# Product 3 of a batch's result in seven block products, in a cross-attention kernel of nested Strassen products

## The chip, the cores and the metric

The kernel runs on one core of a Trainium2 chip, in 32-bit floating point. The time is the device's, in microseconds, from the start to the end of one execution. The kernel before took 664.79 us (median of three runs, 664.58 to 664.88).

## The reference

Eight batches are computed with the same weights. x1 and x2 hold 512 channels x 1024 positions per batch.

```python
q = einsum('bcn,dc->bnd', x1, Wq) + bq          # 64 wide
k = einsum('bcn,dc->bdn', x2, Wk) + bk[:, None]
v = einsum('bcn,dc->bdn', x2, Wv) + bv[:, None] # 512 channels
attn = softmax(einsum('bnd,bdm->bnm', q, k), axis=2)
out = einsum('bcm,bnm->bcn', v, attn) + x1
```

## The kernel before, in words

The kernel does not form v. It multiplies x2 by the transposed exponentials of the scores first, y = x2 . e, scales y by one over the sums, and then takes the result, Wv . y + bv + x1. Both large products of a batch, y and the result, are cut into 2 x 2 blocks and done in seven products instead of eight (the Winograd form of Strassen's scheme, `MULT`, L436). The left sums S1 to S4 and the right sums T1 to T4 that they need are built by VectorE, by ScalarE with an accumulating transfer (a negation on ScalarE, then a transfer on POOL's queue that adds the other summand), or by transfers alone. Products 1, 6, 7, 5, 3 and 4 share two pairs of PSUM banks, "a" and "c"; between them ScalarE copies the partial sums of products 1, 6, 5 to buffers `tmp` that the four blocks 11, 12, 21, 22 are put together from (`evict_y`, `evict_o`).

Most of the fourteen products are themselves done in seven block products (L537 `right_stream` and L522 `left_stream` build the sums, `inner_product`, L548, issues the matmuls). Such a product uses a PSUM bank `chain` and a bank `third`: block product 1 starts the chain and is copied by ScalarE to the first half of a bank; 6 and 5 go on with the chain and are copied too; 2, 3 and 4 are added into the copies; block product 7 goes to `third`, is copied to SBUF, and VectorE adds it to the second bank at the end (`complete`, the join). A block product is one matmul of 256 columns for the result and two for y. A plain product of the result is four matmuls of 512 columns.

In the middle batches the result's products run in this order on TensorE: 4 of y and 1 of the result woven together (`multiply_41`, L788), 6 and 2 plain, then 5, 7 and 3 woven (`multiply_57`, L674; 7 in blocks, 5 and 3 plain), then 4 plain. Product 3 goes into banks "a", on top of 1, 6 and 5; block 12 is evicted from these banks by two activations of ScalarE (L930) while product 4 runs. Then the next batch begins: its product 1 of y (`multiply_seeded`, L723), 2, 6, its next batch's scores, 5, 7, 3. Only in the last batch is product 3 of the result done in blocks (`multiply_573`, L588).

All orders are written out by hand: `period(s, n, nn, nnn)` (L1168) issues the work of batch s together with that of the following ones, with `manual_schedule`. Each engine runs its instructions in the order of the program. `weave` (L492) takes operations from several streams in turn. VectorE's streams at the end of a batch are: the subtraction of the maxima from the next batch's scores (`lower`, L320; one call is one score tile of a half, 128x1024), the right sums of products 7 of the result and 1 and 2 of the next y, left sums, T1, the joins and the evictions of blocks 22 and 21; then T2 and the sums of the next batch's product 6. SP's queue carries plain loads and stores. POOL's queue carries all accumulating transfers: sums of score tiles (`add_tile`, L966), S2 and S3 (`add_11`, L181), S4 (L160), T3 (L366), T4 (L361), and the addition of x1 to a block of the result before SP stores it (L942, L943).

In the code batches count from 0 and `s.six` marks 2 to 5, so these are batches 3 to 6 here; `s.b` is the number, and `n` the batch that follows.

Of the kernel before, what the change touches and what calls it, by code (L numbers as in the profile page):

```python
# [15 lines left out]
def kernel(  # L16
# [77 lines left out]

    def load_values():
# [28 lines left out]
    class Batch:  # L124
        def __init__(self, b):
            self.b = b
            self.a, self.e, self.t, self.y, self.o = {}, {}, {}, {}, {}
            self.mx, self.top, self.den, self.few, self.rden, self.row = {}, {}, {}, {}, {}, {}
            self.tmp, self.bank = {}, {}
            self.inner = {}  # L130
            self.six = 2 <= b < B - 2
            self.one = b >= 1

# [438 lines left out]
    def left_values(i, k):  # L572

        x = w[k]
        inner_w[i] = v = {f"{p + 1}{q + 1}": x[:, q : q + 1, ts(p, P)] for p in range(2) for q in range(2)}
        if i == "o3":
            sums = sb.tile([P, 4, 1, P], F32, tag="aS1", name=f"w_I{k}")
        else:
            sums = const.tile([P, 4, 1, P], F32, name=f"w_I{k}")
        for z, (k, x, y, op) in enumerate(LEFT):  # L580
            v[k] = sums[:, z]
            nc.vector.tensor_tensor(v[k], v[x], v[y], op)
            yield
# [89 lines left out]
    def multiply_57(s, hook):  # L673
# [10 lines left out]
        s.tmp[5] = sb.tile([P, 2, H], F32, tag="u5", name=f"uo5_{s.b}")  # L684

# [36 lines left out]

    def multiply_seeded(s, i, v_tag, hooks={}, bank=None):  # L723
# [10 lines left out]
        chain, third = inner_parts(s, i)  # L734
        if v_tag == "top" or s.b == B - 1 and v_tag == "r":
# [172 lines left out]
    def evict_o(s, k, hook=None, rows=range(2)):  # L908
# [5 lines left out]
        if s.b == B - 1 and k == "12":  # L914
            bank = "d"
        r, h = int(k[0]) - 1, int(k[1]) - 1
# [94 lines left out]
    def head(s):  # L1011
# [13 lines left out]
        warm = const.tile([P, P], F32, name="warm")  # L1025
# [86 lines left out]
    def period(s, n, nn, nnn):  # L1112
# [122 lines left out]
        else:  # L1235
            complete_1 = multiply_seeded(s, 1, "y11", {4: lambda: copied_s4(s)} if s.b > 1 else {})
            early = s.b > 1 and n is not None
            complete_1()
            sum_e(s, *(("T2",) if early else ("T1", "T2")))
# [42 lines left out]
            if early:  # L1282
# [8 lines left out]
            if n:  # L1291
                weave(left_stream(s, 7, s.a["S3"], "yT4"))
            if s.six:
# [55 lines left out]
            sums_4 = (left_stream(s, 4, s.a["22"], "a12"), right_stream(s, 4, s.t["T4"], "eT2"))  # L1349
# [49 lines left out]
        if five:  # L1399
# [3 lines left out]
            highest(n, 1)  # L1403
            next(products, None)
            if nn is None:
# [15 lines left out]
        if five:  # L1421
            if nn is None:
# [3 lines left out]
                in_turn(lowers(n, 0, 2, MH), lowers(n, 1, 0, 2)),  # L1426
                right_stream(s, "o7", s.y["T3"], "eT1"),
# [18 lines left out]
        if five:  # L1446
# [14 lines left out]
        if n is None:  # L1461
            weave(left_values("o3", "S4"))
# [23 lines left out]
        if n is None:  # L1486
            pass
        elif late:
# [3 lines left out]
        if n:  # L1492
            leave = evict_o(s, "22")
        if five:
            exponentials(n, 1, 3)
# [6 lines left out]
        if five:  # L1502
# [4 lines left out]
        if n:  # L1507
            weave(
                in_turn(
                    right_stream(n, 1, n.e[0][:, 0], "yT1", "yT2"), right_stream(n, 2, n.e[0][:, 1], "eT4")  # L1510
                ),
                left_stream(n, 2, n.a["12"], "aI3" if n.b > 1 else "aS4"),
            )
            if s.b == 0:
                second(3)
            last = evict_o(s, "12")
            if five:
# [3 lines left out]
            second(4)  # L1521
            total(n, 0)
            evict_o(s, "21")
# [45 lines left out]
```

## Time and profile before

| | |
|---|---|
| median of three runs | 664.79 us (664.58 to 664.88) |
| the profiled execution's own time | 664.86 us |
| its span, from the first to the last instruction of the program | 662.8 us |
| granted TensorE clock | 1.00 |
| transfers in the span | 135.88 MB |

PE is TensorE's matmuls, PEld its weight loads, DVE VectorE, ACT ScalarE, POOL GpSimd, SP the synchronisation engine. A row of a timeline gives the start in us from the span's start, the duration, the engine, the line of the kernel, the operation, what it writes and reads (tile names without their numbers), the shape and a count. Durations of neighbours on one engine overlap, so the spacing of starts is what one costs. A bracket tells how long the engine was idle before it and what ended that. The names: `i1chain`, `i6third` and the like are the banks of y's block products; `io7chain` those of the result's product 7; `e` the exponentials, `eT` their sums, `a` and `aS` the parts of x2 and their sums, `aI` the inner left sums, `y` and `yT` the blocks of y and their sums, `oa` and `oc` the banks of the result, `uo`, `r` and `o` its blocks in SBUF.

### The profile page before, as it was taken

To read this page: it belongs to the slowest core of one execution; us is meant where nothing else is said; L and a number is where in the kernel's file an instruction comes from. 1 tells how busy PE (TensorE), PEld (TensorE's weight loads), DVE (VectorE), ACT (ScalarE), POOL (GpSimd) and SP (SyncE) were. 2 spreads that over 40 slices of the span, in tenths; PEclk is the share of its full clock that TensorE was granted. 3 is DMA by queue.
4 is the path that set the end of the run, shared out by engine and by line. 5 is a ranking of instruction groups with operands and counts; after the bars stand their busy time and mean duration, and the time that the engine had idled before them with its cause. 6 is when DMAs were issued, how large, how long until landed. Compare 5 with 4: busy or idle time off the path is not lost.

```text
span 662.8 us, 7971 instructions
## 1 busy us (share of the span) xinstructions
PE 657.8 (99%) x2620; PEld 432.4 (65%) x2620; DVE 615.9 (93%) x865; ACT 378.2 (57%) x723; POOL 224.1 (34%) x192
## 2 busy tenths in 40 slices
PE   9999999999999999999999999999999999999997
PEld 4435754757658666687666786676865757666865
DVE  1989999999999989998999989999899999999997
ACT  3755456446475574655756647656577555574332
POOL 0125215631255411563125531265214640244300
PEclk9999999999999999999999999999999999999999
DMA  9688587995899859999599985999947995399504
GB/s 327 260 274 261 126 247 136 197 229 199 263 167 227 238 169 285 174 233 239 166 279 186 259 222 164 257 194 234 279 87 173 207 256 190 75 183 240 125 23 150
DMA packets 51545, 135.88 MB, mean 205 GB/s; under 512 B 5680, under 2 KB 6192, under 8 KB 51504
## 3 DMA queue, kind: packets, MB, share of 16 engines
q0 software_dynamic: 24512, 61.94, 50.7%
q1 hardware_dynamic: 26848, 73.29, 30.5%
q8 instruction: 21, 0.34, 0.2%
q10 hardware_dynamic: 144, 0.14, 0.1%
q14 instruction: 20, 0.16, 0.1%
HBM read 87.83 MB, written 16.81 MB: 158 GB/s over the span
## 4 chain that ended last, share of the span: by engine, by line
PE 98%; DMA 1%; DVE 0%; issue 0%
PE ps_yc L555 9%; PE ps_oc L464 8%; PE ps_ya L555 7%; PE ps_s L236 6%; PE ps_oa L689 6%; PE ps_oa L464 5%; PE ps_ya L464 4%; PE ps_q L191 4%; PE ps_i5chain L555 3%; PE ps_i4b L840 3%; PE ps_k L191 3%; PE ps_i3chain L555 3%; PE ps_i7chain L555 3%; PE ps_oc L840 3%; PE ps_i2chain L555 3%; PE ps_i1chain L555 3%
## 5 line engine op out<-in xcount | busy, mean ns | idle before, releaser
L331 ACT ACTIVATE e<-e 128x1024 f32<-128x1024 f32 x60 | 63.4, 1058 | 30.2 <-DVE e L322 29.2
L322 DVE TENSOR_TENSOR e<-e,top 128x1024 f32<-128x1024 f32 x60 | 72.6, 1218 | 2.5 <-POOL top L272 2.5
L291 POOL PARTITION_ALL_REDUCE den<-sum x16 | 52.8, 3298 | 63.9 <-DVE sum L266 59.0
L272 POOL PARTITION_ALL_REDUCE top<-max x16 | 29.9, 1867 | 97.0 <-DVE max L266 50.0
L966 POOL DMA_DIRECT2D sum<-e x21 | 25.6, 1219 | 102.9 <-ACT sum L971 39.1
L245 ACT COPY e<-ps_s 128x512 f32<-128x512 f32 x90 | 47.8, 622 | 10.1 <-PE ps_s L236 7.1
L236 PE MATMUL ps_s<-q,k 64*128 64x512 f32 (+1 forms) x188 | 46.6, 598 | 0.0
L256 DVE TENSOR_TENSOR max<-max,e 128x1024 f32<-128x1024 f32 x30 | 36.6, 1219 | 0.3
L236 PEld LDWEIGHTS ps_s<-q,k 64*128 64x128 f32 x188 | 17.5, 186 | 19.9 <-issue 17.0
L875 DVE TENSOR_TENSOR y<-y,den 128x1024 f32<-128x1024 f32 x24 | 29.2, 1221 | 0.3
L464 PE MATMUL ps_oa<-yT,w_S 128*128 128x512 f32 x64 | 28.8, 593 | 0.0
L464 PE MATMUL ps_oc<-yT,w 128*128 128x512 f32 x64 | 28.8, 592 | 0.0
L746 ACT COPY ps_yc<-ps_i7chain 128x256 f32<-128x256 f32 x32 | 11.4, 357 | 30.2 <-PE ps_i7chain L555 26.1
L307 POOL DMA_DIRECT2D den<-row x12 | 6.7, 559 | 58.7 <-DMA row<-few 39.2
L522 DVE TENSOR_TENSOR aI<-a,aI 128x256 f32<-128x256 f32 x60 | 25.2, 420 | 0.6
L522 DVE TENSOR_TENSOR aI<-a 128x256 f32<-128x256 f32 x60 | 25.8, 450 | 0.0
L191 PE MATMUL ps_q<-x_in_x_dram,wqk_sb 128*64 128x512 f32 x112 | 25.6, 598 | 0.0
L746 ACT COPY ps_ya<-ps_i5chain 128x256 f32<-128x256 f32 x32 | 11.5, 361 | 24.2 <-PE ps_i5chain L555 20.0
L746 ACT COPY ps_ya<-ps_i1chain 128x256 f32<-128x256 f32 x28 | 10.0, 357 | 24.3 <-PE ps_i1chain L555 20.6
L555 PE MATMUL ps_yc<-e,aI 128*128 128x256 f32 x92 | 23.6, 379 | 0.0
L689 PE MATMUL ps_oa<-yT,w_S 128*128 128x512 f32 x48 | 23.5, 592 | 0.0
L942 POOL DMA_DIRECT2D r<-in_x_dram x14 | 23.3, 1664 | 0.0
(348 smaller groups left out, 1836.9 us busy)
## 6 DMA issues: line engine op xcount, KB each, us to landing
x_in_x_dram<-in_x_dram SPq DMA_DIRECT2D x60, 512.0 KB, 8.2
a<-in_x2T_dram SPq DMA_DIRECT2D x32, 512.0 KB, 7.2
aS<-in_x2T_dram POOLq DMA_DIRECT2D x21, 512.0 KB, 10.5
sum<-e POOLq DMA_DIRECT2D x21, 512.0 KB, 5.3
eT<-eT POOLq DMA_DIRECT2D x16, 512.0 KB, 11.7
uo<-in_x_dram POOLq DMA_DIRECT2D x14, 512.0 KB, 9.9
r<-in_x_dram POOLq DMA_DIRECT2D x14, 512.0 KB, 9.0
out_dram<-r SPq DMA_DIRECT2D x14, 512.0 KB, 7.6
```

Of the source, the lines that this page charges most:

```text
L191: nc.tensor.matmul(ps[r, :], w_sb[:, c, :], s.x[:, c, ts(h, H)], start=(c == 0), stop=(c == CT - 1),)
L236: nc.tensor.matmul(ps[g][:, n], s.k[r, ts(i, P)], s.q[r, ts(h, H)][:, n], start=True, stop=True)
L245: nc.scalar.copy(e[:, g, i, :], ps[g])
L256: nc.vector.tensor_tensor(f, e[:, :, 0, :] if i == 1 else f, e[:, :, i, :], op)
L291: nc.gpsimd.partition_all_reduce(s.den[h], s.mx[h][:, 0, :], P, ReduceOp.add)
L322: nc.vector.tensor_tensor(e, e, top, ALU.subtract)
L331: nc.scalar.activation(e, e, AF.Exp)
L464: nc.tensor.matmul(ps, left[ka][:, k, ts(j, P)], right[kb][:, k, :], start=opens and k == 0, stop=i in (2, 3, 4) and k == n_k - 1, skip_gr ...
L522: nc.vector.tensor_tensor(v[k], v[x], v[y], op)
L555: nc.tensor.matmul(ps, s.inner[i][ka][:, k, :], s.inner[i, "t"][kb][:, k, :], start=opens and k == 0, stop=z in (2, 3, 4) and k == n_k - 1 ...
L689: nc.tensor.matmul(ps, w[ka][:, k, ts(j, P)], s.y[kb][:, k, :], start=False, stop=i == 3 and k == 1, skip_group_check=True,)
L840: nc.tensor.matmul(ps, s.inner[i][ka][:, k, :], s.inner[i, "t"][kb][:, k, :], start=opens and k == 0, stop=z in (2, 3, 4) and k == n_k - 1 ...
```

## The change

In batches 3 to 6 product 3 of the result is done in seven block products, woven with 5 and 7 in a new function, `multiply_573_early`. It has two banks of its own, `d`, from the pool of four that `chain` and `third` also come from. Block 12 is then in two parts: banks "a" (products 1, 6, 5) are evicted with the bias to `r12` right behind the seven products; the banks `d` are copied to SBUF by ScalarE (`evict_3`) and added to `r12` by a transfer on POOL's queue. The right sums of product 3 (`sums_o3`) and its left sums (`left_values("o3", "S4")`, once, in batch 3) are added to VectorE's work.

Product 4 of the result is issued inside the next batch's product 1 of y, behind its block product 7, with what belonged to it: S3's negation and transfer, block 22's transfer and store; batch total and the eviction of block 21 come behind block product 2. The right sums of the next batch's product 1 are issued ahead of the join of product 7, and those of product 2 partly behind product 1.

Moved besides: the subtraction and the exponential of score tile 2 of half 0 go earlier (ahead of `join_67`, and behind product 4 of y); the left sums of product 4 of y go ahead of product 5's join; product 5's third part goes into the tile `u5`; the inversion of half 0 goes behind product 7's left sums. The inner left sums of `w11` are partly held in place and in the tile `warm`.

```diff
+            self.three = 2 <= b < B - 2
...
+        if s.three:
+            return multiply_573_early(s, hook, b0, b1, chain, third)
...
+    ORDER573_EARLY = (
+        (5, 0), (5, 1), (7, 1), (7, 7), (5, 2), (3, 7), (3, 1), (7, 6), (7, 2), (3, 2), (3, 6),
+        (5, 3), (7, 5), (3, 4), (3, 5), (7, 4), (7, 3), (3, 3),
+    )
+    def multiply_573_early(s, hook, b0, b1, chain, third):
+        d = [ps_s.tile([P, H], F32, tag="s", name=f"ps_od{j}_{s.b}_3") for j in range(2)]
+        v = sb.tile([P, H], F32, tag="top", name=f"vo73_{s.b}", bufs=2)
+        v7, v3, copy = v[:, left], v[:, right], nc.scalar.copy
+        s.r12 = sb.tile([P, 2, H], F32, tag="r", name=f"r12_{s.b}")
+        a0, a1, d0, d1 = ([x[:, left], x[:, right]] for x in (b0, b1, *d))
+        steps = {
+            (7, 1): (chain, True, [(a0[0], chain)]),
+            (7, 7): (third, True, [(v7, third)]),
...
+            (7, 4): (a1[0], False, [(a1[1], chain)]),
+            (7, 3): (a0[1], False, []),
+            (3, 7): (d1[1], True, []),
+            (3, 1): (d1[0], False, [(d0[0], d1[0]), (v3, d1[1])]),
...
+        for j in range(2):
+            nc.scalar.activation(s.r12[:, j, :], s.bank["a", j], AF.Identity, bias=bv_sb[j])
+        def complete():
+            for b, v in ((b1, v7), (d[1], v3)):
+                b = b.rearrange("p (a n) -> p a n", a=2)
+                nc.vector.tensor_tensor(b, b, v.unsqueeze(1).to_broadcast([P, 2, H // 2]), ALU.add)
+                yield
...
+    def evict_3(s, n):
+        t = sb.tile([P, 2, H], F32, tag="y21", name=f"t3_{s.b}")
+        nc.scalar.copy(t[:, 0, :], s.d[0])
+        exponential(n, 1, 3)
+        nc.scalar.copy(t[:, 1, :], s.d[1])
+        nc.gpsimd.dma_start(s.r12, t, accum_op=ALU.add)
...
-            complete_1 = multiply_seeded(s, 1, "y11", {4: lambda: copied_s4(s)} if s.b > 1 else {})
+            hooks = {4: lambda: copied_s4(s)} if s.b > 1 else {}
+            if s.tail:
+                hooks[7] = lambda: (negate(s, "S3"), add_11(s, "S3"), s.tail[0]())
+                hooks[2] = s.tail[1]
+            complete_1 = multiply_seeded(s, 1, "y11", hooks)
             complete_1()
+            if s.tail:
+                s.tail[2]()
...
-            if early:
+            if early and not s.tail:
                 invert(s, 0)
...
+            if s.b == 2:
+                weave(left_values("o3", "S4"))
+            elif s.six:
+                inner_left(s, 4, s.a["22"], "a12")
             complete_5()
...
+            if s.six:
+                lower(n, 0, 2)
             join_67(s)
...
+            if s.six:
+                sums_o3 = right_stream(s, "o3", s.y["22"], "aI3")
+                next(sums_o3)
             next(products, None)
+            if s.six:
+                exponential(n, 0, 2)
...
-                in_turn(lowers(n, 0, 2, MH), lowers(n, 1, 0, 2)),
-                right_stream(s, "o7", s.y["T3"], "eT1"),
+                in_turn(lowers(n, 0, 2 + s.six, MH), lowers(n, 1, 0, 2)),
+                in_turn(right_stream(s, "o7", s.y["T3"], "eT1"), sums_o3),
...
+        elif s.three:
+            sums_n1 = right_stream(n, 1, n.e[0][:, 0], "yT2", "yT1")
+            weave(sums_n1)
+            next(complete_7)
...
+        if s.three:
+            next(complete_7)
+            evict_3(s, n)
...
+            if s.three:
+                n.tail = lambda: (leave(), second(4)), tail, lambda: weave(*sums_n2)
+            else:
+                second(4)
+                tail()
```

More of the change, by code (lines that the diff above doesn't have):

```diff
@@ L93 @@
     }
+    warm = const.tile([P, P], F32, name="warm")
     def load_values():
@@ L915, in evict_o, with leave @@
             bank = "d"
+        if k == "12" and s.three:
+            o = s.r12
+            def leave():
+                nc.gpsimd.dma_start(o, block(s, k, x1), accum_op=ALU.add)
+                nc.sync.dma_start(block(s, k, out), o)
+            return leave
         r, h = int(k[0]) - 1, int(k[1]) - 1
```

87 lines of the change are left out of this document (65 added, 22 removed).

## The prediction

> **What bounds the kernel now.** I read the page first, then the busy time by period, then the timeline of TensorE, and last VectorE, ScalarE and the transfers at the one place that the change touches.
>
> ```profile
> span 662.8 us, 7971 instructions
> PE 657.8 (99%) x2620; PEld 432.4 (65%) x2620; DVE 615.9 (93%) x865; ACT 378.2 (57%) x723; POOL 224.1 (34%) x192
> ...
> q0 software_dynamic: 24512, 61.94, 50.7%
> ...
> PE 98%; DMA 1%; DVE 0%; issue 0%
> ```
>
> ```profile
> 295.04:375.38 80.34, 80.34 (x329) 55.09 (x328) 75.84 (x109) 49.49 (x97) 30.01 (x27) 1.00 0.90 220
> ```
>
> The first fence is the page (its busy times and its chain), the second the row of one period (PE, PEld, DVE, ACT, POOL busy, the granted clock, the DMA share, GB/s). The chain that ended last is 98% PE, and in one period of a middle batch (80.34 us) PE is never idle. So a matmul fewer is worth its time, and nothing else gains anything. But VectorE is busy for 75.84 of the 80.34 us, and the DMA engines are at a share of 0.90. The reader is to see a bound engine with a second and a third right behind it: PE can only run ahead as far as they follow.
>
> The place is the seam of two batches. I work it out for the end of batch 3 and the start of batch 4 (260 to 296 us); the others lie a period further.
>
> ```profile
> 263.80 1.88 PE L689 MATMUL ps_oa<-yT,w_S 128*128 128x512 f32 x4
> ...
> 269.39 0.59 PE L555 MATMUL ps_oc<-eIo7eT,w 128*128 128x256 f32 x2
> ...
> 273.69 3.60 PE L464 MATMUL ps_oc<-yT,w 128*128 128x512 f32 x8
> 277.12 1.03 PE L555 MATMUL ps_i1chain<-e,a 128*128 128x256 f32 x4
> 277.99 1.03 PE L555 MATMUL ps_i1third<-eI1yT,aI 128*128 128x256 f32 x4
> ```
>
> The durations overlap, so the starts count: eight 512-wide instructions take 277.12 - 273.69 = 3.43 us, 0.43 each; four 256-wide ones take 277.99 - 277.12 = 0.87 us, 0.216 each. A matmul in the code is two of these instructions.
>
> **The change, part by part.** *Term 1, TensorE.* Product 3 was four matmuls of 512 columns: 8 x 0.43 = 3.43 us. It becomes seven of 256: 14 x 0.216 = 3.02 us. That saves 0.41 us in each of four batches: **-1.64 us**. No other matmul is added; product 4 changes only its place.
>
> A rule of the Trainium skill speaks against this ("TensorE: Matmul & The Clock Gate", section "The mechanism"): a weight load overlaps matmuls in flight only when its row group differs.
>
> ```profile
> 289.86 0.84 PEld L555 LDWEIGHTS ps_i6third<-eI6yT,aI 128*128 128x128 f32 x4
> 290.74 0.82 PEld L555 LDWEIGHTS ps_i6chain<-eI6y,aI 128*128 128x128 f32 x4
> ```
>
> Here every load fills all 128 rows and takes 0.19 us (the four of a group begin 0.22 apart and end 0.84 after the first began), and four loads with four matmuls still take 0.88 us from group to group: the loads are hidden, and the trace disagrees with the rule. By the rule six more loads a batch would add 4 x 6 x 0.19 = 4.6 us.
>
> *Term 2, VectorE after the seam.* This is where I expect part of the gain to go.
>
> ```profile
> 262.24 0.68 DVE L537 TENSOR_TENSOR eIo7eT<-yT 128x512 f32<-128x512 f32 x1
> 262.84 1.22 DVE L322 TENSOR_TENSOR e<-e,top 128x1024 f32<-128x1024 f32 x1
> 263.98 0.42 DVE L542 TENSOR_TENSOR eIo7eT<-eIo7eT,yT 128x256 f32<-128x256 f32 x1
> 264.31 1.22 DVE L322 TENSOR_TENSOR e<-e,top 128x1024 f32<-128x1024 f32 x1
> ...
> 270.53 0.69 DVE L719 TENSOR_TENSOR ps_oc<-ps_oc,vo 128x512 f32<-128x512 f32 x1
> 271.31 1.41 DVE L937 SCALAR_TENSOR_TENSOR uo<-ps_oc,wqk_sb,uo 128x512 f32<-128x512 f32 x2
> ...
> 273.77 2.43 DVE L340 TENSOR_TENSOR eT<-e,e 128x1024 f32<-128x1024 f32 x2
> 276.12 1.22 DVE L537 TENSOR_TENSOR eI1yT<-e 128x1024 f32<-128x1024 f32 x1
> ...
> 280.94 0.69 DVE L542 TENSOR_TENSOR eI2eT<-eI2eT,e 128x512 f32<-128x512 f32 x1
> 281.66 0.69 DVE L544 TENSOR_TENSOR eI2eT<-e,eI2eT 128x512 f32<-128x512 f32 x1
> ...
> 289.83 0.41 DVE L522 TENSOR_TENSOR aI<-aS,aI 128x256 f32<-128x256 f32 x1
> ```
>
> From 261 to 291 us VectorE runs without a gap; by the starts a 1024-wide operation takes 1.14 us, a 512-wide one 0.60, a 256-wide one 0.33. At 289.83 comes the third left sum of batch 4's product 6; its block product 6 loads it at 290.74, 0.50 us after the sum's end (290.24). That is all the lead VectorE has. What the change does to this streak:
> - the subtraction for score tile 2 leaves it: -1.14; two of the right sums of product 3 come in: +0.67;
> - the join of product 3's third part comes in (512 wide, as the one at 270.53): +0.60;
> - the three right sums of product 1 (1.14 + 0.60 + 0.60) move ahead of the join of product 7. This costs nothing by itself, but now that join waits. It needs the last copy of the seven products, which in the trace starts 0.63 us after block product 4 of product 7 (the row below at 270.02 against 269.39). In the new order four double matmuls and eleven block products lie before that one: 263.80 + 3.43 + 4.73 = 271.97. So the copy runs from 272.60 to 272.96 and the join starts at 272.99, while VectorE is free at 270.53 - 0.47 + 2.34 = 272.40: +0.59. Behind it on VectorE wait block 22's eviction, the last subtraction, T1 and T2;
> - small waits that now have passed: 271.31 - 270.53 is 0.18 above 0.60, T1 took 2.35 instead of 2.28, and 281.66 - 280.94 is 0.12 above 0.60: -0.37.
>
> The sum is +0.35 us: the third left sum ends at 290.59, while PE, 0.41 us earlier, wants to load it at 290.33. With 0.05 us for the signal (below: a sum ending at 260.06 frees a load at 260.11) PE stalls 0.31 us.
>
> ```profile
> 258.83 1.23 DVE L875 TENSOR_TENSOR y<-y,den 128x1024 f32<-128x1024 f32 x1
> ...
> 260.11 0.45 PEld L464 LDWEIGHTS ps_oc<-y,w 128*128 128x128 f32 x2 [0.41 <-DVE y L875]
> ```
>
> Batches 4, 5 and 6 have this product 6 in blocks behind a changed seam: 3 x 0.31 = **+0.9 us**. Bounds: nothing (if the join does not wait), and 3 x 0.9 = 2.7 us (if it waits twice as long).
>
> *Covered edits.* The rest I cost at nothing, with its cover:
>
> ```profile
> DVE ps_ya L763 <- ACT ps_ya L746: 1.5, 1, 1.5
> DVE uy L858 <- ACT uy L863: 1.3, 1, 1.3
> DVE ps_i4b L833 <- ACT ps_i4b L849: 1.0, 1, 1.0
> ```
>
> ```profile
> 269.16 0.58 ACT L698 COPY uo<-ps_oa 128x512 f32<-128x512 f32 x1
> 269.64 0.38 ACT L564 COPY ps_oc<-ps_io7chain 128x256 f32<-128x256 f32 x1
> 270.02 0.36 ACT L711 COPY ps_oc<-ps_io7chain 128x256 f32<-128x256 f32 x1
> 270.29 1.06 ACT L331 ACTIVATE e<-e 128x1024 f32<-128x1024 f32 x1
> 271.25 1.05 ACT L177 ACTIVATE aS<-aS 128x1024 f32<-128x1024 f32 x1
> ...
> 274.85 1.25 ACT L930 ACTIVATE r<-ps_oa,wqk_sb 128x512 f32<-128x512 f32 x2
> 275.99 1.05 ACT L177 ACTIVATE a<-a 128x1024 f32<-128x1024 f32 x1
> ```
>
> VectorE has three gaps in a period. The left sums of product 4 (4 x 0.33) go into the one of 1.5 us, the subtraction of tile 2 into the one of 1.3, the first right sum of product 3 (0.60) into the one of 1.0. ScalarE gets four more 256-wide and two more 512-wide copies a batch, and they meet at the seam: behind the copy of 272.60 (0.27 to the next start) follow the two activations of block 12 (0.57 each), an exponential, S2's negation (0.96 each), a copy (0.48), an exponential, a copy, and only then product 1's first copy, from 277.85 to 278.21. Product 4 (3.43 us), now between block products 7 and 6 of product 1, holds the reader of that copy off until 273.69 - 0.41 + 1.73 + 3.43 = 278.44: covered by 0.2 us, and every tenth beyond that stalls PE a tenth. What product 4 covered before, the eviction of block 12 (L930), is done during the seven products. The value sums are made once, in batch 3, and leave the last batch. With product 4 move S3's negation (0.96 on ScalarE, behind product 1's second copy and before its third, which comes 0.9 us after product 4), the transfers of S3 and of block 22, batch 4's total and block 21's eviction; on POOL S3 now goes ahead of block 22, and SP keeps its order of stores. The inversion of half 0 goes behind product 7's left sums, as the row that it reads comes later. Product 5's third part takes block 22's buffer, whose store goes out before block 12's: I count nothing.
>
> *Transfers.* A batch gets one more accumulating transfer of 0.524 MB: 61.94 MB took 50.7% of 662.8 us, so it is 2.8 us of all 16 engines; at 0.90 of 80.34 us some 8 us are free. On POOL's queue it stands behind the sum into S2 and ahead of T3's two sums, S3's, block 22's, and all behind these come later by about one transfer less what the three earlier ones of tiles 2, 3 and block 11 gained.
>
> **The sum:** -1.64 + 0.9 = -0.7 us on the profiled 664.86 us: 664.1; the median of 664.79 lies 0.1 below, which I can't tell apart. **664.1 us.**
>
> **The rivals.**
> *No stall.* If the join of product 7 doesn't wait (a copy 0.6 us earlier, or faster sums), VectorE stays 0.24 us ahead of the trace and PE 0.41 ahead of it: 0.50 - 0.05 - 0.41 + 0.24 is positive, and all of term 1 stays: 664.79 - 1.64 = 663.2 us. For it: every other lead closes. Against it: the copy stands last in the new order.
>
> *S2 late: slower.* ScalarE makes S2's negation at 271.25; now it stands behind block 12's activations and an exponential and ends at about 275.9, so POOL sends S2's transfer at 276.0, not 272.6.
>
> ```profile
> L181 POOL DMA_DIRECT2D aS<-in_x2T_dram x1: 905/905/905, 272.6 to 272.6; - x1
> DMA to landing us min/median/max: 9.0/9.0/9.0
> ...
> L966 POOL DMA_DIRECT2D sum<-e x1: 1252/1252/1252, 264.3 to 264.3; - x1
> DMA to landing us min/median/max: 4.9/4.9/4.9
> ...
> 282.77 1.06 ACT L156 ACTIVATE aS<-aS 128x1024 f32<-128x1024 f32 x1
> ```
>
> ScalarE reads S2 (L156) for S4, at 282.4 in the new time. If the transfer takes 9.0 us as now, it lands at 285.0; ScalarE, in order, holds product 2's first copy until 286.3, which block product 6 of product 2 wants at 284.5 (277.12 - 0.41, nine steps of 0.865 later): 1.9 us a batch, four times: 664.79 - 1.64 + 7.6 = 670.8 us. It decides from 7.0 us after issue (0.6 us of slack). For it: the one row of this transfer says 9.0. Against it: the three transfers ahead go out some 5 us earlier, and behind an emptier queue one took 4.9 us.
>
> *Loads not hidden:* 24 extra loads of 0.19 us in line with the matmuls give 664.79 - 1.64 + 4.6 = 667.7 us. The rows of PEld speak against it. (The rule of the Trainium skill quoted above would have it so.)
>
> *It does not come to blocks:* the new order is in place for all four batches by the code; I see no way for that.
>
> **How the numbers follow.** Forecast (a stall of 0.1 to 0.6 us in three batches, 663.5 to 665.0 us): 0.48. No stall (663.0 to 663.5): 0.28. S2 late (665.5 to 671): 0.17. A larger stall of the same streak, up to its bound of 2.7 us (665.0 to 666): 0.06. Loads not hidden: 0.01. The range goes from 662.9 to 667.0 and leaves out the upper half and more of S2 late, about 0.12 in all; the likeliest's own range is 663.5 to 665.0. A measurement of this kernel can tell about 0.2%, 1.3 us, from no change. Faster by more needs under 663.5: no stall, 0.28. Slower needs over 666.1: S2 late, the loads and a little of the larger stall, 0.20. Between: 0.52.
>
> **What would show it.** Term 1: in batches 3 to 6 fourteen 256-wide instructions of product 3, and the start of product 1 0.43 us earlier. Term 2: in batches 4 to 6 a start of product 6's block product 6 some 0.3 us late, released by VectorE, and a wait of product 7's join for ScalarE. Wrong: that load without a wait (no stall); ScalarE idle before S4's negation with a DMA as releaser (S2 late); PE waiting for ScalarE at block product 6 of product 1, where my 0.2 us of cover are thin; or 256-wide instructions further apart than 0.216 us.

## The result, and the profile after

The changed kernel took 668.01 us (median of 6 runs, 667.06 to 669.49), the kernel before 664.65 on the same chip (6 runs, 664.40 to 664.88): a ratio of 1.0053, 95% interval 1.0039 to 1.0067. It is slower by about 3.4 us; the forecast was 664.1, with a range to 667.0.

The page of the changed kernel, profiled in an execution of 668.01 us: span, busy times, POOL's queue of transfers, and the chain that ended last.

```profile
span 666.2 us, 8081 instructions
PE 658.8 (99%) x2644; PEld 436.9 (66%) x2644; DVE 629.6 (95%) x881; ACT 386.6 (58%) x747; POOL 230.1 (35%) x196
...
q0 software_dynamic: 25088, 64.04, 51.9%
...
PE 77%; DVE 11%; DMA 6%; issue 3%; POOL 2%; ACT 1%; SPq 0%; POOLq 0%
```

The busy time of one period (columns as before):

```profile
295.78:376.55 80.77, 80.44 (x336) 56.05 (x335) 79.29 (x113) 51.60 (x103) 31.51 (x28) 1.00 0.93 224
```

The chain was 98% PE; now it leaves TensorE for VectorE, transfers and POOL. TensorE's busy share hardly shows this (99% both times): a stall of some tenths lies under the modelled end of the matmul before it. VectorE went from 75.84 to 79.29 us of a period that itself grew from 80.34 to 80.77.

So I compare starts of the same matmul in the two traces. The start of y's product 1 shows term 1 alone: 273.30 us in place of 277.12. With product 4 (3.43 us, now behind it) taken off, that is 0.39 us earlier, and 0.41 with the 0.02 us by which this execution lay behind at 142 us. The same comes at each of the four seams. What comes back is at two kinds of place:

- into batches 4, 5 and 6: 0.83 us at each seam, so each is +0.42 in all;
- in batch 7: 2.55 us.

-1.64 + 3 x 0.83 + 2.55 = +3.40 us, which is the difference of the spans (666.2 - 662.8).

**The seam into batch 4.** The timeline of TensorE in the changed kernel:

```profile
273.30 1.03 PE L559 MATMUL ps_i1chain<-e,a 128*128 128x256 f32 x4
...
283.63 1.03 PE L559 MATMUL ps_i2third<-eI2eT,aI 128*128 128x256 f32 x4
284.84 1.13 PE L559 MATMUL ps_i2chain<-eI2eT,aI 128*128 128x256 f32 x4 [0.17 <-ACT ps_yc L821]
...
290.12 1.03 PE L559 MATMUL ps_i6third<-eI6yT,aI 128*128 128x256 f32 x4
291.30 0.89 PE L559 MATMUL ps_i6chain<-eI6y,aI 128*128 128x256 f32 x3
```

Between groups that follow without a wait lie 0.865 us. Here are 1.21 and 1.18: 0.34 and 0.31 us late, and 0.10 and 0.07 us more between the first two matmuls of each late group (the bracket shows only what the modelled ends leave of it). Into batches 5 and 6 both waits are in product 6, and both for VectorE. VectorE at the same place:

```profile
273.02 0.70 DVE L780 TENSOR_TENSOR ps_oc<-ps_oc,vo 128x512 f32<-128x512 f32 x1
...
281.81 0.69 DVE L270 TENSOR_TENSOR sum<-sum 128x512 f32<-128x512 f32 x1
282.41 1.40 DVE L1020 SCALAR_TENSOR_TENSOR o<-ps_oc,wqk_sb,uo 128x512 f32<-128x512 f32 x2
283.73 0.69 DVE L838 TENSOR_TENSOR ps_ya<-ps_ya,v 128x512 f32<-128x512 f32 x1
284.33 1.47 DVE L548 TENSOR_TENSOR eI2eT<-e,eI2eT 128x512 f32<-128x512 f32 x1
...
290.74 0.41 DVE L526 TENSOR_TENSOR aI<-aS,aI 128x256 f32<-128x256 f32 x1
```

The third left sum of product 6 is the row at 290.74; it ends at 291.15, not at the forecast 290.59. The row that does not fit is the one at 284.33: a 512-wide sum of 1.47 us, where the same sum of the same width took 0.69 in the trace of before. It waits for nothing that the profile names.

**Batch 7.** ScalarE, TensorE and VectorE of the changed kernel, each from its timeline:

```profile
551.99 0.37 ACT L821 COPY v<-ps_i7third 128x256 f32<-128x256 f32 x1 [2.53 <-DMA out_dram<-o]
```

```profile
552.68 1.13 PE L559 MATMUL ps_i7chain<-eI7yT,aI 128*128 128x256 f32 x4 [1.03 <-ACT ps_yc L821]
569.16 0.67 PE L915 MATMUL ps_oc<-eIo1i,w 128*128 128x256 f32 x2 [0.36 <-DVE yT L943]
579.38 2.84 PE L468 MATMUL ps_oc<-y,w 128*128 128x512 f32 x6 [0.30 <-DVE y L950]
```

```profile
558.21 1.23 DVE L950 TENSOR_TENSOR y<-y,den 128x1024 f32<-128x1024 f32 x1 [1.28 <-DMA den<-row]
```

Two late transfers stand behind it. The third part of product 7 goes to the tile `y12`, in which block 21's result still waits for its store. And the reciprocals of the softmax sums, sent to DRAM as a row and read back to all partitions, come late, so that VectorE can't scale y. By the starts TensorE loses 1.29 us at the store, 0.36 at the scores behind it, and 0.60 and 0.57 at the last two rows of the TensorE fence; 0.27 us that the kernel before lost inside product 4 of y at this place fall away. That makes the 2.55 us.

### The profile page after: what moved, and what is told of

Read it like the earlier page. It is cut to its first block, busy times and chain, and to the rows that moved or that the text cites. A ratio compares the mean times of both kernels' runs of the same rounds, so it can differ in the third digit from the quotient of the medians.

```text
span 666.2 us, 8081 instructions
## 1 busy us (share of the span) xinstructions
PE 658.8 (99%) x2644; PEld 436.9 (66%) x2644; DVE 629.6 (95%) x881; ACT 386.6 (58%) x747; POOL 230.1 (35%) x196
## 4 chain that ended last, share of the span: by engine, by line
PE 77%; DVE 11%; DMA 6%; issue 3%; POOL 2%; ACT 1%; SPq 0%; POOLq 0%
PE ps_yc L559 7%; PE ps_s L240 6%; PE ps_ya L559 5%; PE ps_oc L468 5%; PE ps_oa L468 4%; PE ps_q L195 4%; PE ps_k L195 3%; PE ps_ya L468 3%; PE ps_i5chain L559 3%; PE ps_i7chain L559 3%; PE ps_i3chain L559 3%; PE ps_i4b L915 3%; PE ps_oc L915 2%; PE ps_i4chain L915 2%; PE ps_oa L695 2%
## 5 line engine op out<-in xcount | busy, mean ns | idle before, releaser
L295 POOL PARTITION_ALL_REDUCE den<-sum x16 | 54.4, 3401 | 52.4 <-DVE sum L270 47.5
L276 POOL PARTITION_ALL_REDUCE top<-max x16 | 32.7, 2046 | 99.9 <-ACT ps_oa L928 52.3
L468 PE MATMUL ps_oa<-yT,w_S 128*128 128x512 f32 x64 | 28.8, 593 | 0.0
L526 DVE TENSOR_TENSOR aI<-a,aI 128x256 f32<-128x256 f32 x60 | 27.4, 456 | 1.0
L468 PE MATMUL ps_oc<-y,w 128*128 128x512 f32 x48 | 21.7, 594 | 0.3 <-DVE y L950 0.3
L195 PE MATMUL ps_k<-x_in_x_dram,wqk_sb 128*64 128x512 f32 x96 | 21.9, 598 | 0.0
L468 PE MATMUL ps_ya<-eT,aS 128*128 128x512 f32 x48 | 21.1, 592 | 0.0
## 6 DMA issues: line engine op xcount, KB each, us to landing
aS<-in_x2T_dram POOLq DMA_DIRECT2D x21, 512.0 KB, 10.5
eT<-eT POOLq DMA_DIRECT2D x16, 512.0 KB, 11.9
uo<-in_x_dram POOLq DMA_DIRECT2D x14, 512.0 KB, 10.5
```

The lines of the kernel that those rows point to most:

```text
L195: nc.tensor.matmul(ps[r, :], w_sb[:, c, :], s.x[:, c, ts(h, H)], start=(c == 0), stop=(c == CT - 1),)
L276: nc.gpsimd.partition_all_reduce(s.top[h], s.mx[h][:, 0, :], P, ReduceOp.max)
L295: nc.gpsimd.partition_all_reduce(s.den[h], s.mx[h][:, 0, :], P, ReduceOp.add)
L468: nc.tensor.matmul(ps, left[ka][:, k, ts(j, P)], right[kb][:, k, :], start=opens and k == 0, stop=i in (2, 3, 4) and k == n_k - 1, skip_gr ...
```

## The experiments

A number such as "+0.42" below is the change of TensorE's start against the kernel before, across one seam or batch of the profiled execution. The first 53 us, in which all kernels here are the same program, end between 0.3 us earlier and 1.4 us later than in the profile of before (waits for the first loads). That blurs the medians; the starts across a seam don't have this. In seam_6's profiled execution (671.88 us, 5.3 over its median) TensorE lies 5.65 us behind before batch 3, where nothing is changed yet, so of that trace I use only what comes later. The first theory was VectorE's amount of work for the seams, and the transfers for batch 7; the rival put the transfers behind both.

**seams_345** and **seam_6**: the change in batches 3 to 5 alone, and in batch 6 alone.

```diff
-            self.three = 2 <= b < B - 2
+            self.three = 2 <= b < B - 3        # seams_345; parts of the change that asked s.six ask s.three
+            self.three = b == B - 3            # seam_6
```

> The change in batches 3 to 5 only; batch 6 ends and batch 7 begins as before. Two theories of the loss. VectorE theory: each seam into a batch with product 6 in blocks (4, 5, 6) loses 0.83 us to VectorE's streak and wins 0.41, and batch 7 loses 2.6 us by its own seam's transfers; then here 664.65 + 3 x 0.42 = 665.9 us, and no wait in batch 7. Transfer theory (everything goes back to the added transfer): the same seams, so 665.9 too. Rival: batch 7's loss is a lag carried over from the batches before it; then it stays, and the time is 664.65 + 1.3 + 2.6 = 668.5 us.

> The change in batch 6 only, so that its seam leads into batch 7, which has no product 6 in blocks. VectorE theory and transfer theory: 0.41 won at the seam, about 2.6 lost in batch 7 (ScalarE waits for the store of block 21, VectorE for the row of the sums): 664.65 - 0.41 + 2.6 = 666.8 us. If batch 7's loss is carried over from earlier batches: 664.2 us.

Measured: 666.42 (ratio 1.0023, 1.0011 to 1.0036) and 666.57 us (1.0030, 1.0009 to 1.0052). seams_345: +0.42 at each of its three seams and no loss in batch 7. seam_6: -0.41 at the seam; batch 7 loses 0.53 us at product 2, where ScalarE had waited 1.07 us for S2's transfer, and 0.61 and 0.91 us behind the late row; the wait for the store of block 21 was not there. So batch 7's loss belongs to the seam just ahead of it.

**no_add**: without the accumulating transfer of product 3 to block 12 (the output lacks that part). **no_join**: with it, but without VectorE's join of product 3's third part (the output lacks that).

```diff
-        nc.gpsimd.dma_start(s.r12, t, accum_op=ALU.add)          # no_add
-            for b, v in ((b1, v7), (d[1], v3)):                  # no_join
+            for b, v in ((b1, v7),):
```

> The change without the accumulating transfer of the copied banks to block 12: product 3 is computed and copied, but left out of block 12. VectorE theory: the seams lose 0.83 us each as before (their streak holds the same operations), only batch 7's loss shrinks, to 0 to 0.5 us: 664.65 - 1.64 + 2.5 + (0 to 0.5) = 665.5 to 666.0 us. Transfer theory: with 2.8 us of transfer work less per batch the seams lose nothing either: 664.65 - 1.64 = 663.0 us.

> The change without VectorE's addition of product 3's third part (its block product 7 is left out of half of block 12); all transfers stay. VectorE theory: the streak is 0.60 us shorter per seam, so the stall at product 6 in batches 4 to 6 falls from 0.83 to about 0.2 us each: 668.0 - 1.9 = 666.1 us, batch 7 as in the change. Transfer theory: no difference, 668.0 us.

Measured: no_add 664.17 us (0.9987, 0.9979 to 0.9996), between the theories: 0.0 at each of the three seams, -0.41 at the last, no loss in batch 7. no_join 668.25 us (1.0046, 1.0031 to 1.0062), as the rival had it: the three seams still +0.42 each, although VectorE had a join of 0.60 us less to do, and batch 7 loses 2.29 us, all of it at the wait for the store. With that the theory of VectorE's amount fell. At the seam into batch 4, about 0.32 us of the time saved went into a wait of VectorE for an exponential of ScalarE (two sums start 1.45 us apart in place of 1.13). What had become of the rest shows where VectorE meets POOL. First no_join, then no_add, each with POOL's all-reduce of the batch total and the VectorE sum that the row at 284.33 above showed:

```profile
283.50 3.91 POOL L295 PARTITION_ALL_REDUCE den<-sum  x1
```

```profile
285.23 1.74 DVE L548 TENSOR_TENSOR eI2eT<-e,eI2eT 128x512 f32<-128x512 f32 x1
```

```profile
282.45 3.23 POOL L295 PARTITION_ALL_REDUCE den<-sum  x1 [0.27 <-DVE sum L270]
```

```profile
284.18 1.05 DVE L548 TENSOR_TENSOR eI2eT<-e,eI2eT 128x512 f32<-128x512 f32 x1
```

POOL's queue in the changed kernel:

```profile
278.27 0.86 POOL L794 DMA_DIRECT2D r<-t  x1 [1.00 <-ACT ps_ya L821]
278.82 2.08 POOL L370 DMA_DIRECT2D e<-e  x2
279.90 1.90 POOL L185 DMA_DIRECT2D a<-in_x2T_dram  x1
280.44 2.60 POOL L1025 DMA_DIRECT2D uo<-in_x_dram  x1
282.60 3.65 POOL L295 PARTITION_ALL_REDUCE den<-sum  x1
```

And the kernel before, where the held operation was T2 (two of 1024 columns, 2.35 us where nothing holds them):

```profile
283.05 3.23 POOL L291 PARTITION_ALL_REDUCE den<-sum  x1 [3.52 <-DVE sum L266]
```

```profile
284.79 2.72 DVE L340 TENSOR_TENSOR eT<-eT,e 128x1024 f32<-128x1024 f32 x2
```

Take what a held row has over its free duration, and add it to its start: that is when it was let go.

| kernel | let go | the all-reduce ends | between |
|---|---|---|---|
| before | 284.79 + 0.37 = 285.16 | 286.28 | 1.12 |
| changed | 284.33 + 0.78 = 285.11 | 286.25 | 1.14 |
| no_add | 284.18 + 0.36 = 284.54 | 285.68 | 1.14 |
| no_join | 285.23 + 1.05 = 286.28 | 287.41 | 1.13 |

So a new theory: while the all-reduce runs, VectorE can't do this sum until 1.13 us before its end, however early it comes to it. The two evictions and the join ahead of it, which read PSUM and one large operand in SBUF, run inside the all-reduce at their usual 0.60 to 0.66 us; the held ones read two operands in SBUF. The Trainium skill says this ("SBUF — State Buffer", section "Who interferes with whom"): a VectorE instruction with two SBUF inputs contends with a GpSimd instruction that reads SBUF. By the same page of the Trainium skill (section "SBUF: two separate sides") the one that starts first gets the shared pair of ports for the whole instruction, and the other fully blocks. The rows agree on who is held. On how long they differ: the sum is let go 1.13 us before the row of the all-reduce ends, in each kernel of the table. The profile's page calls spans on POOL rough, so what the all-reduce does in these 1.13 us stays open.

By this theory the end of the all-reduce sets the streak, and POOL's queue sets the all-reduce: in the changed kernel and in no_join it stands behind five issues, in no_add behind four, and there it waited for VectorE's own sum (the bracket of 0.27). The rival stayed: the landing of the transfers.

**no_total**: seams_345 without the all-reduce of the batch total. **pool_22_late**: seams_345 with block 22's accumulating transfer behind that all-reduce (its store then also goes behind that of block 21). **pool_22_no_join**: the same, without the join of product 3's third part.

```diff
-        nc.gpsimd.partition_all_reduce(s.den[h], s.mx[h][:, 0, :], P, ReduceOp.add)   # no_total, half 0
-                n.tail = lambda: (leave(), second(4)), tail, ...                      # pool_22_late
+                n.tail = lambda: second(4), tail, ...
             def tail():
                 total(n, 0)
                 evict_o(s, "21")
+                if s.three:
+                    leave()
```

> The change in batches 3 to 5 only, with the all-reduce of the batch total in the seams into batches 4 to 6 left out (the reciprocals are then those of one partition's sums: the output is wrong); every VectorE instruction and every transfer stays. Theory (held by the all-reduce): the third right sum of product 2 takes 0.69 us again in place of 1.47, so the streak behind it ends 0.78 us earlier, of TensorE's 0.82 us of stalls at product 6 at most 0.05 is left, and each seam comes out at -0.35 to -0.41 in place of +0.42: 666.4 - 3 x 0.78 = 664.1. Rival (VectorE's amount of work, or the landing of S2's transfer): within 0.3 us of 666.4.

> The change in batches 3 to 5 only, with block 22's accumulating transfer issued on GpSimd behind the batch total's all-reduce in place of ahead of it (the store of block 21 then also goes ahead of that of block 22). Theory (VectorE held by the all-reduce): VectorE's third right sum of product 2 took 1.47 us in place of 0.69 and ended 0.45 us ahead of the all-reduce's end in three kernels, so the end of the all-reduce sets the hold; without that issue in front, the all-reduce begins about 0.45 us earlier, as it did without the accumulating transfer, the sum takes about 1.05 us, TensorE's stalls at product 6 fall from 0.82 to about 0.41 us, and each of the three seams comes out at 0.0 in place of +0.42: 666.4 - 1.3 = 665.1. Rival (the transfers: block 22's lands still later): 666.4 or more.

> As the run with block 22's transfer behind the all-reduce, and VectorE's join of product 3's third part left out (block 12 is then wrong). Theory (held by the all-reduce): the work taken from VectorE ahead of the all-reduce moves the total's sum earlier as well, and GpSimd's queue no longer stands in the way, so the whole streak moves up by up to 0.4 us: the last stall of 0.34 + 0.07 us at product 6 goes, each seam stands at -0.41, and the time is 665.1 - 1.2 = 663.9. Where GpSimd's queue still ends last, it stays at 665.1. By VectorE's amount of work alone the same edit would have made 0.42 us a seam in the whole changed kernel too, where it made nothing.

Measured: no_total 665.33 us (1.0005, 0.9996 to 1.0014), pool_22_late 668.92 (1.0060, 1.0047 to 1.0073), pool_22_no_join 668.44 (1.0054, 1.0042 to 1.0066). At the seams the theory holds: no_total has -0.37 or -0.38 at each of the three and 0.04 us of stall left, pool_22_late 0.0 at each, pool_22_no_join -0.28, so that the join's time is worth something once POOL's queue does not stand in front. The timelines of VectorE and TensorE in no_total:

```profile
284.05 0.68 DVE L552 TENSOR_TENSOR eI2eT<-e,eI2eT 128x512 f32<-128x512 f32 x1
```

```profile
289.40 1.03 PE L563 MATMUL ps_i6third<-eI6yT,aI 128*128 128x256 f32 x4
290.26 1.07 PE L563 MATMUL ps_i6chain<-eI6y,aI 128*128 128x256 f32 x4
```

The sum is back at 0.68 us, and product 6 goes on after 0.86. But the medians miss what I expected, by 1.2, 3.8 and 4.5 us. All three lose time at a new place, product 5. ScalarE in pool_22_late:

```profile
306.33 0.37 ACT L821 COPY v<-ps_i5third 128x256 f32<-128x256 f32 x1 [2.02 <-DMA out_dram<-uo]
```

Product 5's third part goes to block 22's buffer (`u5`), and its copy waits for the store of block 22. TensorE loses 0.85, 1.87 and 1.06 us there in pool_22_late, and in no_total nothing, 0.78 and 1.17 (and 0.59 once at the scores, where ScalarE's copies come late). In the changed kernel that store landed at 302.70 in batch 4 and the copy ran at 305.03: 2.3 us of margin. In batch 6 it landed 0.1 us ahead of the copy (466.46 and 466.56), and in batch 5 the copy, at 386.01, already waited for it (landed at 385.91), about 0.2 us, which did not reach TensorE. So little or nothing is left as soon as TensorE runs ahead or the store goes later.

**sp_21_first**: the changed kernel with the store of block 21 ahead of the store of block 22 on SP's queue.

```diff
-                n.tail = lambda: (leave(), second(4)), tail, ...
+                n.tail = lambda: (leave(store=False), second(4)), tail, ...
             def tail():
                 total(n, 0)
                 evict_o(s, "21")
+                if s.three:
+                    leave(add=False)
```

> One reorder of the changed kernel: the store of block 22, which stands on SyncE's queue ahead of the store of block 21 and there waits for block 22's accumulating transfer, is put behind the store of block 21. Theory (SyncE's queue): in the changed kernel the store of block 21 was issued at 540.00 us, right behind that of block 22 at 539.52 (before the change 532.60 and 532.11), and landed at 551.91; batch 7's third part on ScalarE waited for it and TensorE lost 1.2 + 0.1 us there, and the 0.6 and 0.6 us behind it hang on the same queue. Then the store of block 21 is issued near 533 and lands near 543, the wait of 2.5 us on ScalarE is gone, and the time falls by 1.3 to 2.5 us: 665.5 to 666.7. Rival (the transfers' own backlog): the store lands near 551 whenever it is issued, and the time stays within 0.3 us of 668.0.

Measured: 670.29 us (1.0079, 1.0066 to 1.0092): neither, but worse. Batch 7's wait for the store is gone, but 1.90 us of its 2.55 are still lost, behind the late row; the three seams still stand at +0.41 to +0.45. And the store of block 21, issued at 284.27 in place of 296.71, now competes with the accumulating transfers. Block 22's lands at 299.17 in place of 296.17, its store at 307.44 in place of 302.70 (0.42 us of each is the start of that execution), and product 5 waits for it as above, 1.37, 1.16 and 1.10 us. So the order on SP's queue was not the cause; here it kept the store of block 21 out of the way of block 22's transfer.

**pool_22_v5**: pool_22_late with product 5's third part in the tile `y21`, which no store holds. **later_total**: seams_345 with the same tile, and the total (fold and all-reduce) behind the sums of product 6.

```diff
         if s.six and i == 5:
-            v_tag = "u5"
+            v_tag = "y21"                      # both
...
+            if s.tail:                         # later_total; taken out of tail()
+                total(s, 0)
+                complete_2()
+                evict_y(s, "11")
+                total_1(s)
```

> The run with block 22's transfer behind the all-reduce, with the third part of product 5 in a buffer that no store holds. That run lost 0.85, 1.9 and 1.05 us at product 5, each where ScalarE's copy of that third part waited for the store of block 22, and its three seams else came out near 0.0. Theory (the store's landing is the whole loss there): these losses go, the seams stay at 0.0: 668.9 - 3.8 = 665.1, the kernel before within 0.5 us. Rival (the transfers' backlog stops something else next): another wait of the same size at the next user of a late transfer, 667 or more.

> The change in batches 3 to 5 only, with two edits: the batch total (its fold on VectorE and its all-reduce) goes behind the sums of product 6, just ahead of product 2's join and its two evictions, which read PSUM; and the third part of product 5 gets a buffer that no store holds (in place of block 22's). The inversion goes behind the next scores. Theory (VectorE held by the all-reduce): the streak ahead of product 6 loses the fold (0.6 us) and the hold (0.78 us), so no stall is left at products 2 and 6, and each seam comes out at -0.41 in place of +0.42: 666.4 - 3 x 0.83 = 663.9, under the kernel before by 0.9. Against it: the second total's all-reduce then has no evictions beside it and can hold VectorE by up to 2.1 us before product 5; that costs up to 0.4 us a seam if product 5's margin of 1.5 us does not cover it: 665.1. Rival (transfers alone): 666.4.

Measured: pool_22_v5 664.75 us, the kernel before 665.21 on that chip (0.9995, 0.9986 to 1.0003): the losses at product 5 are gone, the three seams stand at 0.0, and 0.18 us are lost once, at product 3 of batch 4. What is left at each is the stall that the last 0.36 us of the hold makes:

```profile
290.55 1.10 PE L559 MATMUL ps_i6chain<-eI6y,aI 128*128 128x256 f32 x4 [0.17 <-DVE aI L526]
```

later_total 666.34 us (1.0011, 1.0003 to 1.0020), a miss. Its seams are at -0.41, each of the three. But the same theory takes it back: now the second all-reduce of the batch has no reader of PSUM beside it. VectorE and POOL in later_total:

```profile
293.11 1.70 DVE L286 TENSOR_TENSOR sum<-e 128x1024 f32<-128x1024 f32 x1
...
295.46 2.80 DVE L526 TENSOR_TENSOR aI<-a 128x256 f32<-128x256 f32 x2
```

```profile
291.50 3.23 POOL L295 PARTITION_ALL_REDUCE den<-sum  x1 [3.00 <-DVE sum L270]
...
295.65 3.31 POOL L295 PARTITION_ALL_REDUCE den<-sum  x1
```

Two 256-wide sums of 0.75 us together took 2.80: held 2.05 us. And 293.11 + (1.70 - 1.21) = 293.60 is again 1.13 before the first all-reduce's end (294.73). (The second of the two sums ends at 298.26; less its own 0.41 us that is 297.85, 1.11 before the second all-reduce's end.) VectorE stays late until product 3, where TensorE waits for ScalarE and that for VectorE's join: 1.18 us in each of two periods; in the third, 0.95 us at the result, where it waits for VectorE to scale y. My margin of 1.5 us at product 5 was enough, but I did not follow the lateness on to product 3.

**tile_7**, **row_7** and **tile_7_row**: the changed kernel with batch 7's product 7 using `y21` for its third part; with the row issued on POOL ahead of the two transfers of T4, as before the change (they are held back behind it); with both.

```diff
-            complete_7 = multiply_seeded(s, 7, "y12")
+            complete_7 = multiply_seeded(s, 7, "y21" if s.b == B - 2 else "y12")   # tile_7
...
             if early and s.tail:
                 invert(s, 0)
+                if not s.six:
+                    add_t4(s)                  # row_7; add_t4 taken out ahead of first(6)
```

> The whole change (batches 3 to 6), with the third part of batch 7's product 7 in a buffer that no store holds, in place of the tile of block 21's result. Theory (the store of block 21 holds it): TensorE's 1.2 + 0.1 us there go, the two stalls behind the late row of reciprocals (0.53 + 0.07 and 0.47 + 0.1 us) stay or grow by up to 0.4: 666.7 to 667.1. Rival (the late row alone sets batch 7's end): it stays at 668.0.

> As the run with the buffer of its own in batch 7, and there the row of reciprocals is issued on GpSimd ahead of the two accumulating transfers of T4, as before the change, in place of behind them. Theory (backlog of accumulating transfers, each about 3 us): the row lands about 5 us earlier, at 548 to 550 us in place of 554.3, so the last two stalls go as well, and only the three seams' +0.42 and the last seam's -0.41 are left: 668.0 - 2.5 = 665.5. Rival (the row waits for its inversion, not for the transfers): as the run with the buffer alone.

> The whole change (batches 3 to 6), with one reorder in batch 7: the row of reciprocals is issued on GpSimd ahead of the two accumulating transfers of T4, as before the change; the third part of product 7 keeps the tile of block 21's result. Theory (two separate causes in batch 7: the store of block 21, worth 1.3 us by itself, and the row behind the accumulating transfers, worth 0.9 us or more): the two stalls behind the row (0.6 and 0.57 us) go, the wait for the store stays: 1.3 us of batch 7's loss is left, 668.0 - 1.2 = 666.8. Rival (the store and the row are one chain, whichever is mended the other shows in full): 668.0, as with the buffer of its own alone (667.7).

Measured: tile_7 667.66 us (1.0040, 1.0028 to 1.0052), tile_7_row 666.08 (1.0012, 1.0003 to 1.0020), row_7 666.39 (1.0020, 1.0006 to 1.0034). In the profiles batch 7 loses 2.04 us in tile_7 (the wait for the store is gone, but the row's loss is all there and larger) and 0.16 in tile_7_row. In row_7 all that the changed kernel lost there is gone:

```profile
550.95 1.03 PE L559 MATMUL ps_yc<-e,a 128*128 128x256 f32 x4
551.82 1.03 PE L559 MATMUL ps_i7chain<-eI7yT,aI 128*128 128x256 f32 x4
```

Product 7 goes on without a wait, 0.87 us after the group before it. What row_7 does lose in batch 7 is 0.38 us at product 2, where ScalarE had waited 0.92 us for S2's transfer. So the order of the row and T4's transfers makes the loss: the row alone costs 2.04 us, and in row_7 the wait for the store went with it. The order does no harm by itself: no_add has it too, its row took 9.8 us, and batch 7 lost nothing. It takes the lateness from the added transfer as well. The row's issue in the changed kernel and in row_7, with its time to landing:

```profile
L305 POOL DMA_DIRECT2D row<-few x1: 1251/1251/1251, 541.9 to 541.9; - x1
...
DMA to landing us min/median/max: 12.4/12.4/12.4
```

```profile
L305 POOL DMA_DIRECT2D row<-few x1: 559/559/559, 540.8 to 540.8; - x1
...
DMA to landing us min/median/max: 6.4/6.4/6.4
```

A transfer of 2 KB took 12.4 us behind two accumulating transfers of 512 KB, 6.4 ahead of them. The store of block 21 in row_7, issued at 539.46, landed at 547.95, in place of 540.00 and 551.91: it too no longer stood beside T4's transfers from their first packets. Seven traces fit this: the store took 8.5 us where the first of T4's transfers was issued 1.7 to 1.9 us after it (seam_6, row_7), 10.5 where 0.7 to 1.1 us after it and behind the row (tile_7_row, all_mended), and 11.9 to 12.7 where 0.6 to 0.8 us after it and ahead of the row (changed, tile_7, no_join). That this is why is argued, not shown. And in tile_7_row it landed at 552.54 in spite of the row's order: that the order alone takes the wait for the store away rests on row_7's one trace.

**all_mended**: the changed kernel with the edits of pool_22_v5 (into batches 4 to 6) and of tile_7_row.

> The whole change (batches 3 to 6) with all edits that took a loss away: into batches 4, 5 and 6 block 22's transfer goes behind the total's all-reduce, product 5's third part and batch 7's product 7 third part have a buffer that no store holds, and batch 7's row goes ahead of the transfers of T4. Theory (VectorE held until 1.13 us before the all-reduce's end, and late stores and rows): the three seams come out at 0.0 each (the hold is still 0.36 us, and costs what term 1 gains), the last seam at -0.41, batch 7 at +0.16: 0.25 us under the kernel before on the same chip, a ratio of 0.9996, which no measurement tells from no change. Rival (the backlog of transfers grows over four seams and stops another reader): 0.5 us or more over the kernel before.

Measured: 664.79 us against 664.87 (0.9999, 0.9991 to 1.0008). The seams are at 0.0, 0.0, 0.0 and -0.41, batch 7 at +0.13, and 0.19 is lost once behind the first seam and once in batch 8, both where TensorE waits for ScalarE. The places where the changed kernel lost time are found; of what it gains, the hold of 0.36 us takes all but the last seam's 0.41 us, and the small losses (0.51 us together) take that too. No version here that computes the whole output beats the kernel before by more than a measurement can tell.

## Why the prediction was wrong, point by point

*Term 1* was right: -0.41 us in each of four batches. The rule on weight loads that spoke against it (the Trainium skill, "TensorE: Matmul & The Clock Gate", "The mechanism") did not come true here either: groups of four loads and four matmuls stay 0.865 us apart.

*Term 2* had the right place, the right releaser and the right size of one part: product 7's join waited for ScalarE and began at 273.02 (forecast 272.99). VectorE itself came to it at 272.86, not at 272.40, which cost nothing, because ScalarE's copy sets that start. **The term was mis-sized**, 0.31 us forecast, 0.83 measured. The third left sum ended 0.56 us later than forecast: 0.41 us of it is the growth of the hold (0.37 to 0.78), and 0.12 a left sum that follows on the one it reads (0.45 us from start to start, 0.33 counted). The step that failed is the list of "what the change does to this streak": it counted VectorE's operations at their free durations, and took the hold of 0.37 us on T2, which lay in the trace of before as a pair of 2.72 us, for part of the pattern. The change put one issue more ahead of the all-reduce on POOL; the hold grew to 0.78 us and met a sum that TensorE waits for. Had I asked why 2.72 was not 2.35, the mechanism was there to be seen.

*Covered edits* is the step that cost most. "The inversion of half 0 goes behind product 7's left sums, as the row that it reads comes later": I costed this at nothing. In batch 7 the move puts the row behind T4's two transfers on POOL's queue, and with the store of block 21 this cost 2.55 us; in row_7's profile the order alone gave it back, but for 0.38 us at another place. "Product 5's third part takes block 22's buffer, whose store goes out before block 12's: I count nothing" held in this kernel by 2.3 us in batch 4 and by 0.1 in batch 6; in batch 5 ScalarE waited already, without cost to TensorE. It fell in six experiments (in row_7 and no_join once each, by 0.28 and 0.26 us).

*Transfers*: "all behind these come later" was right, and I drew nothing from it. Block 22's accumulating transfer landed 7.4 us later ahead of batch 7 (539.47 in place of 532.06; 1.3 us of this TensorE had lost by then). It is that lateness that uses up the margins of the row and of both buffers.

*S2 late* came true in part. S2's transfer landed 7.1 us after its issue, at the point from which it decides (7.0), not 9.0; S4's negation on ScalarE waited 1.0 us for it, and by the releasers of the trace this is the 0.34 + 0.10 us at product 2 into batch 4. In the changed kernel it takes nothing extra: into batches 5 and 6 the seam loses the same 0.83 us in product 6. Into batch 7, which has no product 6 in blocks, it did cost: 0.38 us in row_7 and 0.53 in seam_6, where S2's transfer took 6.9 and 7.2 us. The 1.9 us a batch of this rival came in no trace.

## What to carry to other kernels

Where a bound engine is shadowed by a second one at 95%, cost a change by the stretch between two waits, not by its operations. Look there for rows that take longer than others of the same shape: what holds them is a resource that the change can move. Of a step that is moved "at nothing", follow each of its transfers through its queue to the first reader, in every batch in which the work around it differs; a small transfer behind large accumulating ones is the one to fear.

## What the runs showed of the hardware

- An all-reduce over the partitions on POOL (3.23 us) held VectorE operations with two operands in SBUF until 1.12 to 1.14 us before its end, in five kernels (before, changed, no_add, no_join, later_total); the longest hold was 2.05 us on sums of 0.75 us. Operations that read PSUM ran beside it at their usual pace (0.60 to 0.66 us from start to start). An all-reduce of the maxima (2.22 us) let a held 256-wide sum go 0.89 us before its end (changed kernel, 308.61 us: 1.15 us in place of 0.42).
- After a stall of TensorE the first matmuls lost 0.07 to 0.10 us more.
- Issues on POOL that queue behind one another show growing durations (0.86, then 2.08 for two, 1.90, 2.60 us); the all-reduce behind them then has a row of 3.65 or 3.91 us, where 3.23 is its own time.
- A plain store issued 12 us earlier (sp_21_first) delayed an accumulating transfer by 2.6 us and the store behind it by 4.3 (the start of that execution taken off).
